# The MLP's weights kept in SBUF, the gathered rows in the freed weight buffers, weighing and gating two half steps later

## The chip, the cores and the metric

The kernel runs on one core of one Trainium2 chip. The metric is the device time of one execution in microseconds (us). Everything is float32. The engines are called by the names of the profile: PE (TensorE), DVE (VectorE), ACT (ScalarE), POOL (GpSimd) and SP (SyncE, which here only issues DMAs); the name of an engine with a q behind it is its queue.

## The reference, cut to what matters

```python
x = L0_attn_x                                     # 2 x 2048 tokens of 256 values
xn = layernorm(x)

# left branch: a Mamba mixer with an MLP behind it
h = xn + mamba_mixer(rmsnorm(xn), ...)            # 512 channels, 16 states per channel, scan over 2048 tokens
s = h + silu(rmsnorm(h) @ mlp_w1.T) @ mlp_w2.T    # mlp_w1 1024x256, mlp_w2 256x1024

# right branch: a mixture of 8 experts, two per token
p = softmax(xn @ gate_w + gate_b)
top2 = top_k(p, 2)
g = silu(sum over the two of p_e * (relu(xn @ w1[e] + b1[e]) @ w2[e] + b2[e]))

out = x + s * g
```

## The kernel before, in words

The 4096 tokens are 8 blocks of 512 (index `c`). The scan goes through 256 steps `n`: block `c`, channel group `d` (4 groups of 128 channels), pair of states `g` (8 pairs). A step has two half steps (`q` = 0 and 1). For each step DVE makes the input `b` (L1345, two states at once) and runs two scans into `h` (L1349); ACT makes the decays `da` two steps ahead (L1238) and copies the last state into `hs` (L1275); POOL multiplies `h` by `C` and, in most steps, adds the two states (L1279, L1281); PE adds up `y` three steps behind (L1251).

Around that the rest of the work is woven in by hand, half step by half step. Every engine executes its instructions in the order in which they were written out:

- `draw` gives PE about 2.0 units of other work in each half step, from generators that are asked in the order `pre`, `zs`, `projs`, `chain`, `side`. `chain` is `front`, which makes the projections, convolution and `dt` of the next block. `side` is `all_ffn`: 39 expert tiles of 256 tokens (class `Expert`), then 16 tiles of the MLP (class `Mlp`, two halves `hf` of each block), called here by the names `m0_0` to `m7_1`. A generator that yields "wait" is skipped for the half step.
- `later` holds the work of the other engines that follows on a PE result. `later.put(f, after=k)` runs `f` in `later.run()` `k` half steps later; a use that comes earlier forces it with `later.next()`.

A tile of the MLP goes like this. `run` calls `pair` four times (32 matmuls with `w1`, L854), each followed one half step later by a tanh on ACT (L1013) and again one half step later by a product on DVE (`hidm`, L1015); then `second` eight times (32 matmuls with `w2`, L866) into a PSUM bank `po`. While one tile runs, the weights of the next are loaded: four quarters of `w1` and four of `w2`, 256 KB each, from pools with five buffers (tags "w1" and "w2"). SP issues these loads, and every load waits until its buffer has been read by PE.

Each tile also needs the rows that the experts made for its 256 tokens. `gather` (called from `between`, after a `pair`) issues four indirect DMAs on POOL (L1042) into two tiles `yk`. Then `weigh` scales them with four ACT instructions (L1056) and adds the two on POOL (L1060), `tanh` runs on ACT (L1064) and `gate` on DVE (L1067). When the second matmuls are done, `total` (L1078) and, one half step later, `end` (L1085, L1086) finish the tile on DVE; `end` forces what is still open until `self.gated` holds. The next tile's `gather` comes only after that `end`.

The tiles `yk` share two buffers (tag "yk" of the pool `rows`) with the tiles `ex` that `front` uses in `exp_v` and `log_v` for the `dt` of the next block. The list `pair_of` keeps the two apart: `front` takes it from the first `exp_v` of a pair to its `log_v`, `gather` takes it until `end`, and each waits while the other has it.

Of the kernel before, what the change touches and what calls it, by code (L numbers as in the profile page):

```python
# [9 lines left out]
F32 = mybir.dt.float32  # L10
# [4 lines left out]
NB, L, DM = 2, 2048, 256  # L15
DI, DS, DR, KC = 512, 16, 16, 4
NE, FF, TOPK = 8, 1024, 2
NT = NB * L
P = 128
# [9 lines left out]
JS = TS // P  # L29
# [20 lines left out]
def kernel(  # L50
# [24 lines left out]
    wpool = ctx.enter_context(tc.tile_pool(name="w", bufs=3))  # L75
    hpool = ctx.enter_context(tc.tile_pool(name="hid", bufs=4))
    rows = ctx.enter_context(tc.tile_pool(name="rows", bufs=2))
# [99 lines left out]
    def act_table(name):  # L177

        if table[0] != name:
            nc.scalar.preload_act_table_set(name)  # L180
            table[0] = name
# [86 lines left out]
    moff, rstd, both_norms, _, _, off = (stat[:, 2 + n, :] for n in range(6))  # L268
# [84 lines left out]
    later = Later()  # L353
# [12 lines left out]
    def drop(tag, n):  # L366
        gone.setdefault(tag, set()).add(n)

    expert_rows = []
    pair_of = []  # L370
    held = []

    def ring(tag, bufs):

        n = take(tag)
        later.free(tag, n - bufs)
        return tag, n
# [432 lines left out]
    def quarter_w1(name, a1, h):  # L810
        t1 = wpool.tile([P, KM, FF // 4], F32, tag="w1", name=f"w1_{name}_{h}", bufs=5)
        nc.sync.dma_start(
            t1, a1[:, ts(h, FF // 4)].rearrange("(k p) f -> p k f", p=P)
        )
        return t1

    def quarter_w2(name, a2, h):
        t2 = wpool.tile([P, NH // 4, DM], F32, tag="w2", name=f"w2_{name}_{h}", bufs=5)
        nc.sync.dma_start(
            t2, a2[ts(h, FF // 4), :].rearrange("(c p) d -> p c d", p=P)  # L820
        )
        return t2

    class Ffn:
# [6 lines left out]
        def load_w1(self, h):  # L831
            self.w1.append(quarter_w1(self.name, self.a1, h))

        def load_w2(self, h):
            self.w2.append(quarter_w2(self.name, self.a2, h))
# [36 lines left out]
        def between(self):  # L872
            pass
# [41 lines left out]
    class Expert(Ffn):  # L915
# [6 lines left out]
        def begin(self):  # L922
            i = self.i
            e = nc.sync.value_load(expert_of[0:1, i : i + 1], min_val=0, max_val=NE - 1)
            self.a1 = w1[bass.ds(e, 1)].rearrange("o d f -> (o d) f")
            self.a2 = w2[bass.ds(e, 1)].rearrange("o f d -> (o f) d")
            self.b1 = small.tile([P, NH], F32, tag="b1", name=f"b1_{i}")
            nc.sync.dma_start(self.b1, b1[bass.ds(e, 1)].rearrange("o p c -> (o p) c"))
            self.e = e
            self.row = nc.sync.value_load(  # L930
                row_of[0:1, i : i + 1], min_val=0, max_val=NSLOT - TS
            )

        def rows(self):
            i = self.i
            self.xr = rows.tile([P, JS, DM], F32, tag="xr", name=f"xs{i}", bufs=1)
            nc.sync.dma_start(
                self.xr, xs_d[bass.ds(self.row, TS), :].rearrange("(j p) d -> p j d", p=P)
            )
            return  # L940
            yield
# [18 lines left out]
        def finish(self, po, n):  # L960
            i = self.i
            no = ring("ys", 2)
            expert_rows.append(no)
            ys = rows.tile([P, JS, DM], F32, tag="ys", name=f"ys{i}")
            later.put(
                lambda: nc.vector.tensor_tensor(
                    ys, po, self.b2.unsqueeze(1).to_broadcast([P, JS, DM]), ALU.add
                ),
                n, after=2,
            )  # L970
            later.put(
                lambda: nc.sync.dma_start(
                    ys_d[ts(i, TS), :].rearrange("(j p) d -> p j d", p=P), ys
                ),
                no, after=4,
            )

    class Mlp(Ffn):
        early = False

# [5 lines left out]

        def begin(self):
            pass

        def rows(self):  # L990

# [26 lines left out]
            later.put(tanh)  # L1018

        def between(self):  # L1020
            if not self.yk and not pair_of:
                self.gather()

        def before_second(self):
# [5 lines left out]
        def gather(self):  # L1030

            c, hf = self.c, self.hf
            i0 = c * J + hf * JS
            pair_of.append(self.name)
            yk = self.yk = [
                rows.tile([P, JS, DM], F32, tag="yk", name=f"yk{self.name}_{k}") for k in range(TOPK)
            ]
            for no in expert_rows:
                later.free(*no)
            for j in range(JS):  # L1040
                for k in range(TOPK):
                    nc.gpsimd.indirect_dma_start(  # L1042
                        out=yk[k][:, j, :], out_offset=None, in_=ys_d,
                        in_offset=bass.IndirectOffsetOnAxis(
                            ap=row_y[:, k, i0 + j : i0 + j + 1], axis=0
                        ),
                    )
            self.nxo = ring("ys", 2)
            self.xo = rows.tile([P, JS, DM], F32, tag="ys", name=f"xo{self.name}")
            self.tok = slice(c * T + hf * TS, c * T + (hf + 1) * TS)  # L1050
            nc.sync.dma_start(self.xo, x[self.tok, :].rearrange("(j p) d -> p j d", p=P))

            def weigh():
                for j in range(JS):
                    for k in range(TOPK):
                        nc.scalar.activation(  # L1056
                            yk[k][:, j, :], yk[k][:, j, :], AF.Copy,
                            scale=prob[:, k, i0 + j : i0 + j + 1],
                        )
                nc.gpsimd.tensor_tensor(yk[0], yk[0], yk[1], ALU.add)  # L1060

            def tanh():
                act_table(WITH_TANH)
                nc.scalar.activation(yk[1], yk[0], AF.Tanh)  # L1064

            def gate():
                nc.vector.scalar_tensor_tensor(yk[0], yk[1], 1.0, yk[0], ALU.add, ALU.mult)  # L1067
                self.gated = True

            later.put(weigh, after=3)  # L1070
            later.put(tanh, after=5)
            later.put(gate, after=6)

        def finish(self, po, n):
            x1, yk, xo = self.x1, self.yk, self.xo

            def total():
                nc.vector.scalar_tensor_tensor(po, po, 0.5, x1, ALU.mult, ALU.add)  # L1078
                drop("x1", self.n_x1)
                later.put(end, n)  # L1080

            def end():
                while not self.gated:
                    later.next()
                nc.vector.tensor_tensor(po, po, yk[0], ALU.mult)  # L1085
                nc.vector.tensor_tensor(xo, po, xo, ALU.add)  # L1086
                pair_of.clear()
                later.put(
                    lambda: nc.sync.dma_start(
                        out[self.tok, :].rearrange("(j p) d -> p j d", p=P), xo  # L1090
                    ),
                    self.nxo, after=3,
                )

            later.put(total)
# [338 lines left out]
```

## Time and profile before

| | us |
|---|---|
| median of 3 runs | 1565.81 |
| lowest and highest | 1560.62, 1567.42 |
| the profiled execution | 1572.91 |
| span of its trace | 1571.2 |

| engine | busy us | share of the span |
|---|---|---|
| PE | 1401.4 | 89% |
| DVE | 1247.6 | 79% |
| POOL | 1157.2 | 74% |
| ACT | 920.1 | 59% |

The profiled execution lies 7.1 us above the median, and 1.7 us of it lie outside of the span. The DMA queues moved 265.17 MB, 169 GB/s over the span. Of that the MLP's weights are 2 x 64 loads of 256 KB (33.6 MB). The first instruction of an MLP tile's matmuls starts at 1087 us; everything before is the start, the experts and the scan of blocks 0 to 5.

The shares are means over stages with different limits, and the busy time of PE is modelled, so a full PE in it is not a PE at its peak. A row of the timeline gives the start, the duration, engine, line, operation, tiles, how many instructions were merged, and in square brackets how long the engine had been idle and what ended the wait. A wait for several semaphores is put down to the last of them.

### The profile page before, as it was taken

What the parts mean: (1) busy time and instruction counts of PE and PEld (TensorE: products, weight loads), DVE (VectorE), ACT (ScalarE), POOL (GpSimd) and SP (SyncE); (2) the same over time, 40 slices, a digit from 0 to 9 for tenths busy, and PEclk for the clock granted to TensorE, in tenths of its full rate; (3) what the DMA queues carried; (4) which work ended last, traced back from release to release, by engine and by line L of the source; (5) the groups of instructions that cost most, each with busy time, mean ns of one, the idle gap of its engine ahead of it and who ended that gap; (6) DMA issues with size and microseconds to landing.
All of it is one profiled execution on the core that took longest, in us unless ns stands there. A gap on an engine that the chain in (4) does not pass through costs nothing. (4 is left out here: it accounts for less than half of the span.)

```text
span 1571.2 us, 18477 instructions
## 1 busy us (share of the span) xinstructions
PE 1401.4 (89%) x5246; PEld 985.5 (63%) x5246; DVE 1247.6 (79%) x1362; ACT 920.1 (59%) x1890; POOL 1157.2 (74%) x775
## 2 busy tenths in 40 slices
PE   5745999998999999999999999999898898799767
PEld 3532667765776667667776777667555565567536
DVE  7458898798778977799879777996898696899952
ACT  4735576567655755477657665675566564374423
POOL 2668589867886689679967887688866768677852
PEclk8557999999999999999999999999999989899988
DMA  5576335923494347724763368245832437645312
GB/s 190 187 258 252 111 120 182 327 91 102 141 321 146 96 131 250 256 88 132 234 255 110 118 213 295 87 127 180 314 105 87 143 101 249 214 131 164 96 59 84
DMA packets 203749, 265.17 MB, mean 169 GB/s; under 512 B 21744, under 2 KB 174192, under 8 KB 203648
## 3 DMA queue, kind: packets, MB, share of 16 engines
q1 hardware_dynamic: 197504, 247.21, 48.0%
q0 software_dynamic: 6144, 16.79, 3.2%
q8 instruction: 42, 0.69, 0.2%
q14 instruction: 59, 0.48, 0.1%
HBM read 227.50 MB, written 36.44 MB: 168 GB/s over the span
## 5 line engine op out<-in xcount | busy, mean ns | idle before, releaser
L1279 POOL TENSOR_TENSOR h<-h,C 128x1024 f32<-128x1024 f32 x256 | 609.9, 2384 | 246.3 <-ACT hs L1275 193.9
L1349 DVE TENSOR_TENSOR_SCAN h<-da,hs,b 128x512 f32<-128x512 f32 x384 | 479.7, 1271 | 42.6 <-PE y L1251 17.2
L1238 ACT ACTIVATE da<-dt,a_neg 128x512 f32<-128x512 f32 x512 | 358.0, 718 | 40.3 <-DVE h L1349 39.7
L1251 PE MATMUL y<-h,ident 128*128 128x512 f32 x594 | 304.6, 615 | 30.6 <-POOL h L1279 20.2
L1345 DVE TENSOR_TENSOR b<-du,B 128x1024 f32<-128x1024 f32 x256 | 314.8, 1230 | 18.0 <-DMA B<-bcd 11.1
L854 PE MATMUL phe<-xsTe,w_e 128*128 128x256 f32 x1248 | 290.4, 384 | 12.5 <-ACT hide L954 8.8
L1281 POOL TENSOR_TENSOR h<-h 128x512 f32<-128x512 f32 x215 | 277.9, 1292 | 16.9
L854 PEld LDWEIGHTS phe<-xsTe,w_e 128*128 128x128 f32 x1248 | 238.7, 192 | 80.6 <-issue 26.3
L866 PE MATMUL poe<-w_e,hide 128*128 128x256 f32 x1248 | 288.7, 380 | 0.0
L866 PEld LDWEIGHTS poe<-w_e,hide 128*128 128x128 f32 x1248 | 235.7, 190 | 64.9 <-issue 33.6
L954 ACT ACTIVATE hide<-phe,b 128x256 f32<-128x256 f32 x312 | 129.3, 469 | 128.9 <-PE phe L854 128.7
L1251 PEld LDWEIGHTS y<-h,ident 128*128 128x128 f32 x594 | 113.0, 197 | 119.6 <-issue 63.3
L1349 DVE TENSOR_TENSOR_SCAN h<-da,b 128x512 f32<-128x512 f32 x128 | 151.3, 1211 | 11.1 <-PE y L1251 3.2
L854 PE MATMUL phm<-xsTm,w_m 128*128 128x256 f32 x512 | 130.9, 410 | 22.7 <-DVE hidm L1015 19.9
L854 PEld LDWEIGHTS phm<-xsTm,w_m 128*128 128x128 f32 x512 | 104.1, 205 | 55.0 <-DVE hidm L1015 24.2
L866 PE MATMUL pom<-w_m,hidm 128*128 128x256 f32 x512 | 119.0, 384 | 2.0 <-DVE xom L1086 1.7
L866 PEld LDWEIGHTS pom<-w_m,hidm 128*128 128x128 f32 x512 | 97.7, 193 | 28.6 <-issue 11.0
L459 POOL DMA_INDIRECT xs_d<-xt,slot x64 | 63.9, 998 | 49.8 <-issue 22.2
L1275 ACT COPY hs<-h 128x2 f32<-128x2 f32 x192 | 36.1, 188 | 94.7 <-DVE h L1349 92.3
L1042 POOL DMA_INDIRECT ykm<-ys_d,row_y x64 | 61.4, 960 | 38.9 <-issue 11.7
L1015 DVE SCALAR_TENSOR_TENSOR hidm<-hidm,phm 128x512 f32<-128x512 f32 x64 | 42.7, 671 | 55.6 <-ACT hidm L1013 55.6
L582 DVE SCALAR_TENSOR_TENSOR xc<-px,par_sb,xc 128x512 f32<-128x512 f32 x96 | 71.5, 747 | 17.2 <-ACT xc L574 11.8
(175 smaller groups left out, 1431.6 us busy)
## 6 DMA issues: line engine op xcount, KB each, us to landing
w_e<-in_w SPq DMA_DIRECT2D x312, 256.0 KB
B<-bcd SPq DMA_DIRECT2D x64, 512.0 KB
C<-bcd SPq DMA_DIRECT2D x64, 512.0 KB
w_m<-in_mlp_w1T SPq DMA_DIRECT2D x64, 256.0 KB
w_m<-in_mlp_w2T SPq DMA_DIRECT2D x64, 256.0 KB
xs<-xs_d SPq DMA_DIRECT2D x39, 256.0 KB
ys_d<-ys SPq DMA_DIRECT2D x39, 256.0 KB
b<-in_b SPq DMA_DIRECT2D x39, 128.0 KB
```

The source lines that it names most:

```text
L459: r = nc.gpsimd.indirect_dma_start(out=xs_d, out_offset=bass.IndirectOffsetOnAxis(ap=slot[:, k, i : i + 1], axis=0), in_=x_of(i // J, i % ...
L582: nc.vector.scalar_tensor_tensor(v[:, s : s + T], px, conv_w[:, d, KC - 1 - s : KC - s], v[:, s : s + T], ALU.mult, ALU.add,)
L854: nc.tensor.matmul(ph[:, q, :], self.w1[c0 // 2][:, k, ts(q, P)], self.xT[:, k, :], start=(k == 0), stop=(k == KM - 1),)
L866: nc.tensor.matmul(po[:, j, :], self.hid[c // 2][:, c % 2, ts(j, P)], self.w2[c // 2][:, c % 2, :], start=(c == 0 and j == 0), stop=(c == ...
L954: nc.scalar.activation(hc[:, q, :], ph[:, q, :], AF.Relu, bias=self.b1[:, c0 + q : c0 + q + 1])
L1042: nc.gpsimd.indirect_dma_start(out=yk[k][:, j, :], out_offset=None, in_=ys_d, in_offset=bass.IndirectOffsetOnAxis(ap=row_y[:, k, i0 + j : ...
L1238: nc.scalar.activation(das[n][:, q, :], dts[c, d], AF.Exp, scale=a_neg[:, d, 2 * g + q : 2 * g + q + 1])
L1251: nc.tensor.matmul(ys[c, d], ident, hts[n][:, q, :], start=False, stop=(g == DS // 2 - 1 and q == nq - 1),)
L1279: nc.gpsimd.tensor_tensor(hts[n], hts[n], bct[c, "C", g], ALU.mult)
L1281: nc.gpsimd.tensor_tensor(hts[n][:, 0, :], hts[n][:, 0, :], hts[n][:, 1, :], ALU.add)
L1345: nc.vector.tensor_tensor(inp, dus[c, d].unsqueeze(1).to_broadcast([P, 2, T]), bct[c, "B", g], ALU.mult,)
L1349: nc.vector.tensor_tensor_scan(hts[n][:, q, :], das[n][:, q, :], inp[:, q, :], 0.0 if c % CPB == 0 else hs[c - 1][:, d, 2 * g + q : 2 * g ...
```

## The change

The MLP's eight weight quarters are loaded once, for the first MLP tile, and stay in four of the five buffers of each weight tag. All 16 tiles use them. The fifth buffer of "w1" and the fifth of "w2" become the two tiles `yk`, which are allocated once. `gather` and `end` now keep a list of their own, `yk_taken`, so that `pair_of` belongs to `front` alone. `weigh`, `tanh` and `gate` are due 5, 7 and 8 half steps after the `gather`, where they were due after 3, 5 and 6.

```diff
+    mlp_w, yk_tiles, yk_taken = ([], []), [], []
+
     class Mlp(Ffn):
...
+        def load_w1(self, h):
+            if h == len(mlp_w[0]):
+                mlp_w[0].append(quarter_w1("m", self.a1, h))
+            self.w1.append(mlp_w[0][h])
+
+        def load_w2(self, h):
+            if h == len(mlp_w[1]):
+                mlp_w[1].append(quarter_w2("m", self.a2, h))
+            self.w2.append(mlp_w[1][h])
...
         def between(self):
-            if not self.yk and not pair_of:
+            if not self.yk and not yk_taken:
                 self.gather()
...
-            pair_of.append(self.name)
-            yk = self.yk = [
-                rows.tile([P, JS, DM], F32, tag="yk", name=f"yk{self.name}_{k}") for k in range(TOPK)
-            ]
+            yk_taken.append(self.name)
+            if not yk_tiles:
+                for k in range(TOPK):
+                    yk_tiles.append(
+                        wpool.tile([P, JS, DM], F32, tag=f"w{k + 1}", name=f"yk{k}", bufs=5)
+                    )
+            yk = self.yk = yk_tiles
...
-            later.put(weigh, after=3)
-            later.put(tanh, after=5)
-            later.put(gate, after=6)
+            later.put(weigh, after=5)
+            later.put(tanh, after=7)
+            later.put(gate, after=8)
...
             def end():
                 while not self.gated:
                     later.next()
                 nc.vector.tensor_tensor(po, po, yk[0], ALU.mult)
                 nc.vector.tensor_tensor(xo, po, xo, ALU.add)
-                pair_of.clear()
+                yk_taken.clear()
```

## The prediction

> **What bounds the kernel now.** I read the page first, then a table of stages, the waits of the stage that the change touches, and the timeline where its longest wait lies. The first 1087 us hold no MLP matmul, so only the rest can change. Of the rest, the end of the scan (1510 us) parts two stages. The first two rows below are from that table (length, then busy us and instructions of PE, weight loads, DVE, ACT and POOL, then clock, DMA share and GB/s), the third is from the waits of DVE between 1087 and 1571 us.
>
> ```profile
> 1087.00:1510.00 423.00, 365.31 (x1299) 250.47 (x1298) 362.07 (x353) 220.47 (x432) 308.71 (x202) 0.93 0.49 162
> 1510.00:1571.00 61.00, 44.76 (x174) 34.70 (x174) 14.27 (x21) 17.43 (x36) 14.81 (x17) 0.86 0.19 56
> DVE hidm L1015 <- ACT hidm L1013: 55.6, 14, 13.9
> ```
>
> In the stage of 423 us DVE is busy for 362 and idle for 61. PE looks as full, but eight 128x256 matmuls take 1.73 us at full clock (the chain of waits), and 14 tiles of 64 such matmuls are then only 194 us of PE. DVE, with two scans and one product per step, paces this stage, and its idle time is what can be won. Three gaps carry it: 7.31 us at 1098 (tile m0_0), 9.66 at 1247 (m2_0), 13.87 at 1302 (m3_0). Each is put down to ACT's tanh of `hidm`. The timeline of the third, DVE first, then ACT, then POOL, shows what ACT was held by:
>
> ```profile
> 1300.74 1.27 DVE L1349 TENSOR_TENSOR_SCAN h<-da,hs,b 128x512 f32<-128x512 f32 x1
> 1315.88 0.69 DVE L1015 SCALAR_TENSOR_TENSOR hidm<-hidm,phm 128x512 f32<-128x512 f32 x1 [13.87 <-ACT hidm L1013]
> 1317.00 1.77 DVE L1067 SCALAR_TENSOR_TENSOR ykm<-ykm,ykm 128x512 f32<-128x512 f32 x1 [0.44 <-ACT ykm L1064]
> ...
> 1308.57 0.51 ACT L1056 ACTIVATE ykm<-ykm,prob 128x256 f32<-128x256 f32 x1 [10.83 <-DMA ykm<-ys_d,row_y]
> 1312.72 0.51 ACT L1056 ACTIVATE ykm<-ykm,prob 128x256 f32<-128x256 f32 x1 [2.48 <-DMA ykm<-ys_d,row_y]
> 1315.24 0.60 ACT L1013 ACTIVATE hidm<-phm 128x512 f32<-128x512 f32 x1
> ...
> 1297.52 1.27 POOL L648 TENSOR_TENSOR ls<-ex,ls 128x512 f32<-128x512 f32 x1
> 1302.85 0.99 POOL L1042 DMA_INDIRECT ykm<-ys_d,row_y  x1
> 1306.65 0.94 POOL L1042 DMA_INDIRECT ykm<-ys_d,row_y  x1 [0.30 <-issue]
> 1307.61 2.35 POOL L1279 TENSOR_TENSOR h<-h,C 128x1024 f32<-128x1024 f32 x1
> 1313.30 1.26 POOL L1060 TENSOR_TENSOR ykm<-ykm,ykm 128x512 f32<-128x512 f32 x1 [3.34 <-ACT hs L1275]
> ```
>
> The reader is to see a queue in front of a queue. POOL first does the four `dt` instructions of `log_v` (1297.5 to 1302.7), then issues four gathers (4 x 1.25 us). ACT stands before `weigh` until the rows land, the tanh of the MLP stands behind `weigh`, and DVE, in order, stands before `hidm`. m2_0 is the same picture; at m0_0 POOL was late with its products. ACT waits 38.0 us for gathered rows in this stage, 33.4 of it at these three tiles.
>
> **The change part by part.**
>
> Loads. In the written order 120 SP loads of 256 KB are gone (31.5 MB, against 162 GB/s x 423 us = 68.5 MB moved in the stage) and nothing else in number. In the waits of the stage PE never waits for a weight load; the loads come while the tile before is computed, and that covers them. DVE's only wait by that name is 1.03 us. So I count 0. They can shorten a gather: last issue to arrival took 6.04 us at 1306.65 amid loads, and 2.77 at 1560.60 with little else moving, so 0 to 3.3 us per gather. It counts only where ACT waits for rows, and after the change it mostly doesn't.
>
> Order. `pair_of` no longer parts `front` and `gather`. Half steps, as `later.now` counts them, before -> after: for m2_0 `gather` 430 -> 426, `log_v` 429 -> 427, `weigh` 433 -> 431, `end` 435 -> 433; for m3_0 `gather` 446 -> 442, `log_v` 445 -> 442, `weigh` 449 -> 447, `end` 451 -> 449. For m0_0 `gather` stays at 383, `weigh` 386 -> 388, `end` stays at 391. Now the gathers stand on POOL ahead of the four `dt` instructions, and ACT meets `weigh` five half steps (12 us or more) after them. The stalls for rows should go. What is late next is POOL: the same instructions remain to be done before the addition L1060.
>
> - m2_0. From 426 POOL has: product and addition 3.65, the second L636 1.27, four gathers 5.0, product 2.4, root 1.2, `dt` 5.1, product and addition 3.65, addition L1060 1.27. That is 23.5 us from the 1223.6 at which it starts 426 in the trace, so 1247.2, tanh 0.62, gate at about 1248. DVE would be at 433, two half steps of about 2.5 us before the 1247.1 where it stopped at 435, at about 1242.3. 5 us are left of 9.66 + 0.44.
> - m3_0. From 442 to L1060: 3.65 + 5.0 + 5.1 + 2.4 + 3.65 + 1.27 = 21, about 1 late at the start and 0.6 for the tanh: 22.6. DVE takes 7 half steps of 2.75 = 19.3. 3 us are left of 13.87 + 0.44.
> - m0_0. The rows came at 1104.75. ACT would reach `weigh` about 5 us later than the 1094.9 of before, and no `hidm` is due between 388 and 391, so the 4 to 5 us wait is covered by the two steps of `da` made ahead. But POOL was busy without a break from 1079 to 1128, and DVE cannot leave it far behind (five `h` buffers, PE's sums three steps behind). Between 0 and 7.31 left, I take 2.
>
> Won: (7.31 - 2) + (10.10 - 5) + (14.31 - 3) = 21.7 us.
>
> Later gates. `end` now finds its gate not done, besides m2_0 and m3_0 as before, at m3_1, m5_0, m5_1 and m6_1: the tanh and `gate` are forced two half steps after `weigh`, and DVE waits with the scan behind it. Nearest rows: the gate's waits on ACT were 0.43 to 0.80 us. Upper end: POOL one step behind, product and addition 3.65 + L1060 1.27 + tanh 0.62 = 5.5. I take 1 each, near the rows: -4. A new `gather` follows `end` in the same half step as before, so POOL waits no longer than before.
>
> Tail. For m7_0 `weigh` now comes at its forced `end`. ACT had the second tanh of m7_1 done at 1553.0; then four `weigh` 1.7, L1060 1.3 (with its wait 1.4), tanh 0.63, gate 0.69: 1557.5, where the gate before ended at 1556.07. The gather of m7_1 waits for it, and its rows, L1060, tanh and gate set the end (gate 0.43 behind ACT at 1565.92). -1.5.
>
> Port. `gate` reads two SBUF tiles. The timeline shows it, and `du` (L1342), at very different lengths:
>
> ```profile
> 1122.40 4.62 DVE L1342 TENSOR_TENSOR du<-dt,xc 128x512 f32<-128x512 f32 x1
> 1222.55 0.69 DVE L1342 TENSOR_TENSOR du<-dt,xc 128x512 f32<-128x512 f32 x1
> 1135.56 0.67 DVE L1067 SCALAR_TENSOR_TENSOR ykm<-ykm,ykm 128x512 f32<-128x512 f32 x1
> 1418.98 2.28 DVE L1067 SCALAR_TENSOR_TENSOR ykm<-ykm,ykm 128x512 f32<-128x512 f32 x1 [0.80 <-ACT ykm L1064]
> ```
>
> The 14 gates of the stage took 17.6 us, 1.26 each. The Trainium skill, "SBUF — State Buffer", section "Who interferes with whom", says that a DVE instruction with two SBUF inputs and a GpSimd instruction that reads SBUF cannot run together: whichever is second waits for the whole of the first. The 4.62 us lie over two products of POOL (4.67), as the rule has it. It speaks against this change, which moves the gates into a tighter schedule of POOL. By the rule at its worst, a product of 2.38 before each gate, 14 x (2.38 + 0.67 - 1.26) = -25 us, all that is won. By the trace only the chance of meeting POOL rises, from (308.7 + 12.6 of gather gaps) / 423 = 76% to 79%: -0.3 us. I take the trace, since gates met a busy POOL before as well.
>
> Sum: 21.7 - 4 - 1.5 - 0.3 = 16 us. Against the profiled execution 1572.9 - 16 = 1557; that one ran 7.1 above the median of 1565.8, which gives 1550.
>
> **The rivals.**
> - More is won: POOL's backlog doesn't hold DVE and the gates wait for nothing. 31.7 less 1.5: 1535 to 1541. For it: POOL is idle for a quarter of the stage. Against: it is full just there.
> - The gain is spent: PE's products for `y`, or `out_proj` and its x1, stop DVE instead (DVE waited 9.4 us for L762 in the stage). 0 to 7 us won: about 1562.
> - Slower: the forced gates. Six ends come two half steps behind `weigh`, each needing ACT, POOL, ACT and DVE in a row. The gross gain of 31.7 less 1.5 is gone when they cost 5.0 us each. At 7 us each (POOL a step and a half behind) 6 x 7 + 1.5 - 31.7 = +12: 1578. For it: in the stage ACT stood before the tanh four times until POOL had added. Against: those waits were 3.3 us in all, 0.9 at most.
> - That the weights are not kept is excluded by the written order, which has four loads each.
>
> **How the numbers follow.** The sum 0.62, more won 0.16, spent 0.15, slower 0.07. Half a percent, 7.8 us, is about what a measurement of this kernel can tell from no change. Faster is the first two: 0.78; same 0.15; slower 0.07. The residues (0 to 7.3 at m0_0, 1 to 5.5 for each of four gates) spread the first case over 1541 to 1558. With most of the second and third the range is 1535 to 1563.
>
> **What would show it.** ACT's wait for gathered rows in the stage falls from 38 to under 10 us; DVE's idle from 61 to about 45; its gap for `hidm` at m2_0 and m3_0 turns into waits for the tanh L1080 (L1064 before). The rate of DMA in the stage falls by almost half, with no wait of PE gone by that. The last gate comes 1.5 us later against PE's end. I'd be wrong if those gaps were still there under another name, or if forced gates waited 5 us.

## The result and the profile after

| | before | after |
|---|---|---|
| median of 14 runs each, same chip | 1561.15 us | 1551.4 us |
| lowest and highest | 1551.53, 1567.42 | 1544.34, 1554.43 |
| the profiled execution | 1572.91 us | 1551.53 us |
| its span | 1571.2 us | 1549.8 us |

The ratio of the medians is 0.9938, with a 95% interval of 0.9917 to 0.9958: the change saves 9.7 us, between 6.6 and 13.0. The two profiled executions lie 21.4 us apart, more than the change is worth: the one of before is slower than each of the 14 timed runs. The traces let the rest be set aside. I cut each into four at three instructions that both have: the first product `b`, the first MLP matmul, the end of the last scan.

| part (us) | before | after | saved |
|---|---|---|---|
| start to the first `b` | 101.4 | 86.6 | 14.9 |
| first `b` to the first MLP matmul | 985.6 | 985.5 | 0.1 |
| first MLP matmul to the end of the scan (the stage) | 424.3 | 414.2 | 10.1 |
| end of the scan to the end (the tail) | 59.9 | 63.5 | -3.6 |

The first part holds the same work in both and is no effect of the change (the eight traces of the experiments below take 86.3 to 88.0 us for it, too). What the change did is 10.1 - 3.6 = 6.5 us in this pair of executions, just under the low end of the interval.

The table of stages for both kernels, cut at the same instructions, first before and then after (columns as in the prediction: length, then busy us and instructions of PE, weight loads, DVE, ACT and POOL, then clock, DMA share, GB/s):

```profile
1087.04:1511.30 424.26, 366.56 (x1301) 251.24 (x1300) 363.37 (x354) 220.47 (x432) 308.71 (x202) 0.93 0.49 162
1072.10:1486.30 414.20, 359.53 (x1301) 246.86 (x1300) 361.35 (x354) 220.38 (x432) 307.02 (x202) 0.95 0.28 95
```

The instruction counts of the engines agree, and the rate of DMA has fallen from 162 to 95 GB/s. DVE's idle time has gone from 60.9 to 52.9 us: 8.0 of the 10.1 us are waits. The other 2.0 are DVE's own 354 instructions, which took 361.35 us where they had taken 363.37 (more on this under "Port" below). The waits of DVE in this stage, before:

```profile
DVE hidm L1015 <- ACT hidm L1013: 36.7, 7, 13.9
DVE pom L1078 <- PE pom L866: 3.3, 1, 3.3
DVE ykm L1067 <- ACT ykm L1064: 1.7, 3, 0.8
```

and after:

```profile
DVE pom L1094 <- PE pom L866: 14.3, 6, 4.5
DVE yk L1083 <- ACT yk L1080: 12.9, 5, 4.7
DVE hidm L1028 <- ACT hidm L1026: 6.9, 3, 4.7
```

The reader is to see one wait become three. 41.7 us with these names have become 34.1: the wait for `hidm` is down by 30, but 11 of it came back at `total` (L1094) and 11 at `gate` (L1083). ACT's wait for gathered rows, which was 38.0 us, is 1.9 in this stage.

Where it worked is m3_0. DVE, ACT and POOL after, in the lines that answer to those of the prediction:

```profile
1284.90 0.69 DVE L1094 SCALAR_TENSOR_TENSOR pom<-pom,x1m 128x512 f32<-128x512 f32 x1
1289.86 2.17 DVE L1083 SCALAR_TENSOR_TENSOR yk<-yk,yk 128x512 f32<-128x512 f32 x1 [3.09 <-ACT yk L1080]
...
1280.32 1.69 ACT L1072 ACTIVATE yk<-yk,prob 128x256 f32<-128x256 f32 x4
1289.20 0.63 ACT L1080 ACTIVATE yk<-yk 128x512 f32<-128x512 f32 x1 [5.87 <-POOL yk L1076]
...
1275.76 0.95 POOL L1058 DMA_INDIRECT yk<-ys_d,row_y  x1 [0.30 <-issue]
1276.73 1.29 POOL L648 TENSOR_TENSOR ls<-ex,ls 128x512 f32<-128x512 f32 x1
1287.89 1.27 POOL L1076 TENSOR_TENSOR yk<-yk,yk 128x512 f32<-128x512 f32 x1
```

The gathers now stand ahead of the `dt` instructions (L648), ACT's four `weigh` run in one piece without a wait, and what is late is POOL's addition L1076. The gap of 13.87 us is one of 3.09.

How far after is ahead of before, measured from the first MLP matmul to the `b` of each scan step, shows where the stage's 10.1 us come from:

| scan steps | what lies there | ahead at the end of it | change |
|---|---|---|---|
| 184 to 206 | m0_0, m0_1, m1_0 | 0.3 | +0.3 |
| 206 to 207 | gate of m1_1 | -4.3 | -4.6 |
| 207 to 213 | m2_0 | -0.3 | +4.0 |
| 213 to 216 | gate of m2_1 | -4.3 | -4.0 |
| 216 to 222 | m3_0 | 6.9 | +11.2 |
| 222 to the end | m3_1 to m7_0 | 10.1 | +3.2 |

(At single steps the figure also swings by several us and back, where a block of work only moved by a few steps; the rows end where such swings are small. m1_1's gate itself stands ahead of step 206 in before, where it took 0.67 us, and behind it in after. With the same work on both sides the first two rows are -0.4 and -3.9.)

One trace is one execution. The runs E4 and E7 below have the same instructions on DVE as after in this stage up to block 7, and their stages took 410.9 and 410.4 us. They agree with the table within 0.5 us but for two places of 1.7 us: the wait before `total` of m1_1 (4.49 us in after, 2.78 in both) and the gate of m2_1 (4.72 and 3.02 to 3.03). So m2_0's row reads +5.7 or +5.8 there and m2_1's -2.4, and a difference of 3 to 4 us between two single stages means nothing by itself.

### The profile page after: what moved, and what is told of

The parts are those of the page before. It is cut to its first block, busy times and chain, and to the rows that moved or that the text cites. A ratio compares the mean times of both kernels' runs of the same rounds, so it can differ in the third digit from the quotient of the medians.

```text
span 1549.8 us, 18158 instructions
## 1 busy us (share of the span) xinstructions
PE 1396.0 (90%) x5246; PEld 982.9 (63%) x5246; DVE 1244.3 (80%) x1362; ACT 919.8 (59%) x1890; POOL 1154.8 (75%) x775
## 5 line engine op out<-in xcount | busy, mean ns | idle before, releaser
L1365 DVE TENSOR_TENSOR_SCAN h<-da,hs,b 128x512 f32<-128x512 f32 x384 | 479.0, 1271 | 42.7 <-PE y L1267 17.6
L854 PE MATMUL phe<-xsTe,w_e 128*128 128x256 f32 x1248 | 290.8, 385 | 13.5 <-ACT hide L954 8.9
L1297 POOL TENSOR_TENSOR h<-h 128x512 f32<-128x512 f32 x215 | 276.4, 1286 | 16.9
L1365 DVE TENSOR_TENSOR_SCAN h<-da,b 128x512 f32<-128x512 f32 x128 | 151.2, 1210 | 11.2 <-PE y L1267 3.2
L854 PE MATMUL phm<-xsTm,w_m 128*128 128x256 f32 x512 | 125.2, 397 | 21.4 <-DVE hidm L1028 20.8
L854 PEld LDWEIGHTS phm<-xsTm,w_m 128*128 128x128 f32 x512 | 100.6, 198 | 48.9 <-DVE hidm L1028 25.9
L1058 POOL DMA_INDIRECT yk<-ys_d,row_y x64 | 61.6, 962 | 38.6 <-DVE pom L1101 21.3
L966 DVE TENSOR_TENSOR ys<-poe,b 128x512 f32<-128x512 f32 x39 | 26.6, 682 | 58.8 <-PE poe L866 51.9
```

What stands on the lines that cost most here:

```text
L854: nc.tensor.matmul(ph[:, q, :], self.w1[c0 // 2][:, k, ts(q, P)], self.xT[:, k, :], start=(k == 0), stop=(k == KM - 1),)
L1058: nc.gpsimd.indirect_dma_start(out=yk[k][:, j, :], out_offset=None, in_=ys_d, in_offset=bass.IndirectOffsetOnAxis(ap=row_y[:, k, i0 + j : ...
L1297: nc.gpsimd.tensor_tensor(hts[n][:, 0, :], hts[n][:, 0, :], hts[n][:, 1, :], ALU.add)
L1365: nc.vector.tensor_tensor_scan(hts[n][:, q, :], das[n][:, q, :], inp[:, q, :], 0.0 if c % CPB == 0 else hs[c - 1][:, d, 2 * g + q : 2 * g ...
```

## The experiments

Each is one core's whole program and is compared with the kernel before on its own chip, where that one had a median of 1561.46 us (E1 to E4) or 1561.95 us (E5 to E8). Stage and tail are cut as above.

| | median us | ratio to before, 95% | stage | tail |
|---|---|---|---|---|
| E1 weights kept, nothing else | 1560.71 | 0.9996 [0.9986, 1.0005] | 421.0 | 61.8 |
| E2 after with the delays of before | 1548.28 | 0.9911 [0.9893, 0.9929] | 412.7 | 60.7 |
| E3 after with gather and `front` coupled | 1564.78 | 1.0021 [1.0009, 1.0033] | 423.0 | 62.9 |
| E4 after with the traffic put back | 1551.87 | 0.9932 [0.9913, 0.995] | 410.9 | 63.6 |
| E5 after with less work for POOL at m0_0 | 1545.27 | 0.989 [0.9865, 0.9915] | 407.2 | 61.4 |
| E6 E2 with the mean square earlier | 1544.87 | 0.989 [0.9866, 0.9913] | 413.2 | 60.8 |
| E7 after with old delays in the last block | 1548.67 | 0.9922 [0.99, 0.9943] | 410.4 | 61.9 |
| E8 E6 with E5's edit | 1540.1 | 0.9863 [0.9837, 0.9889] | 409.6 | 60.8 |

### E1 to E4: which part of the change carries the gain

**E1**, before with the two overrides alone:

```diff
+    mlp_w = ([], [])
...
+        def load_w1(self, h):
+            if h == len(mlp_w[0]):
+                mlp_w[0].append(quarter_w1("m", self.a1, h))
+            self.w1.append(mlp_w[0][h])
...
+        def load_w2(self, h):
+            if h == len(mlp_w[1]):
+                mlp_w[1].append(quarter_w2("m", self.a2, h))
+            self.w2.append(mlp_w[1][h])
```

> Only the weights are kept: yk, pair_of and the delays 3, 5, 6 stay as before. The stage is counted from the first MLP matmul to the end of the last scan (before 424.3 us, after 414.2), the tail from there to the end (59.9 and 63.5). Theory 'order' (the gain came from moving gather and weigh): no wait of PE was for a load, so the stage stays at 421 to 425, the tail at 60, the gaps of DVE before hidm at m0_0, m2_0, m3_0 stay near 7, 10 and 14 us, time within 4 us of before. Theory 'loads' (less DMA traffic and an emptier SP queue bring the rows sooner): stage 414 to 418 and the gaps shrink to half.

Measured: no difference (0.9996). The rate of DMA in the stage is 93 GB/s, as low as in after, and the waits of before are still there. DVE at m0_0, m2_0 and m3_0 in E1:

```profile
1096.17 1.28 DVE L1027 SCALAR_TENSOR_TENSOR hidm<-hidm,phm 128x512 f32<-128x512 f32 x2 [5.44 <-ACT hidm L1025]
1248.70 0.69 DVE L1027 SCALAR_TENSOR_TENSOR hidm<-hidm,phm 128x512 f32<-128x512 f32 x1 [8.76 <-ACT hidm L1025]
```

The third was 9.96. Each is shorter than in before (7.31, 9.66, 13.87). The rows do come earlier with less traffic: from the last gather's issue to the last `weigh` of the tile it is 3.24, 2.81 and 2.77 us at these three, where it was 5.09, 3.68 and 6.07. But the order that makes ACT wait for them is unchanged, and ACT's wait for rows is still 36.5 us. E1's stage is 3.3 us shorter than before's in the two traces; by the medians, 31.5 MB of loads are worth nothing that this measurement can tell (0.75 us less, and the interval of the ratio includes 1).

**E3**, after with `gather` bound to `pair_of` again, so that kept weights and late delays remain:

```diff
-            if not self.yk and not yk_taken:
+            if not self.yk and not pair_of:
...
-            yk_taken.append(self.name)
+            pair_of.append(self.name)
...
-                yk_taken.clear()
+                pair_of.clear()
```

> After, with gather and front parted by pair_of again (yk in the fifth buffers, weights kept, delays 5, 7, 8): the delays alone. Theory 'delays carry it': the rows are there when ACT comes to weigh, stage 414 to 418. Theory 'the free gather carries it': at m2_0 and m3_0 end now forces weigh itself, so DVE waits for rows, weigh, POOL's addition and tanh in a row; stage 424 to 432, tail 63, no faster than before.

Measured: slower than before by 3.3 us (1.0021, interval above 1), and by 4.1 than E1, from which it differs in the delays and in where the rows lie. The stage, 423.0, is a little under the 424 to 432 that was expected of a free gather that carries the gain. At m2_0 and m3_0 its gates are forced behind the rows. DVE at m2_0 in E3:

```profile
1246.98 0.69 DVE L1028 SCALAR_TENSOR_TENSOR hidm<-hidm,phm 128x512 f32<-128x512 f32 x1 [5.95 <-ACT hidm L1026]
1252.12 0.69 DVE L1083 SCALAR_TENSOR_TENSOR yk<-yk,yk 128x512 f32<-128x512 f32 x1 [4.44 <-ACT yk L1080]
```

5.95 and 4.44 us are 10.4 together, where E1 loses 8.76 and 0.44: without the earlier gather the delay only divides the wait over two instructions.

**E2**, after with the three delays of before:

```diff
-            later.put(weigh, after=5)
-            later.put(tanh, after=7)
-            later.put(gate, after=8)
+            later.put(weigh, after=3)
+            later.put(tanh, after=5)
+            later.put(gate, after=6)
```

> After, with weigh, tanh and gate at 3, 5 and 6 half steps again; weights kept and gather free of front. No gate is forced but those of block 7. Theory 'delays carry it' (as the prediction had it for m0_0): ACT meets the rows too early again, 7 us at m0_0 and some 3 to 5 at m2_0 and m3_0, stage 418 to 424, tail 60, slower than after or equal. Theory 'the free gather carries it, the delays cost': the gates at m1_1, m2_1, m3_0 no longer wait behind ACT's other work, stage 404 to 412, tail 60, faster than after by 6 to 14 us.

Measured: 13.2 us under before, 3.1 under after by the medians, where the two intervals overlap. It did not become the 6 to 14 us that the second theory had forecast. So the whole gain comes from the gather that no longer waits for `front`; of the three edits, the kept weights serve to make room for it, and the two half steps bring nothing on balance. E2 does not lose what after loses at the gates of m1_1 and m2_1, but it gives the same back later: behind step 222 after gains 3.2 us on before (E4 and E7 3.2 and 3.7), and E2 loses 1.5. ACT still waits 23.7 us for rows in E2's stage, so that wait as a whole is not what costs the time.

**E4**, after with every load that it leaves out replaced by a copy of the same quarter from HBM to HBM, 120 in all, issued by SP at the same places:

```diff
+    def copy_of(w, shape, rule, **k):
+        t = dram.tile(shape, F32, tag="copy", name=f"copy{take('copy')}", bufs=16)
+        nc.sync.dma_start(t, w.rearrange(rule, **k))
...
                 mlp_w[0].append(quarter_w1("m", self.a1, h))
+            else:
+                copy_of(
+                    self.a1[:, ts(h, FF // 4)], [P, KM, FF // 4], "(k p) f -> p k f", p=P
+                )
```

(and the same for `w2`).

> After, with 120 copies of the same weight quarters from HBM to HBM in place of the 120 loads that went: SP's queue and the traffic as before (read and written), without a buffer to wait for. It computes the same. Theory 'order': rows have five half steps to arrive, so the stage stays within 3 us of after (414) and the tail within 2 of 63.5. Theory 'loads': 420 or more.

Measured: 1551.87 us, as after. The rate of DMA in the stage is back to 172 GB/s, and no time with it. With E1 this closes the question of the loads from both sides, as far as the medians can tell.

### E5 and E6: the two waits that the prediction sized or named wrongly

In after, m0_0 still loses as much as in before. DVE at m0_0, then ACT's tanh there:

```profile
1095.59 0.70 DVE L1094 SCALAR_TENSOR_TENSOR pom<-pom,x1m 128x512 f32<-128x512 f32 x1 [4.54 <-PE pom L866]
1098.59 2.16 DVE L1083 SCALAR_TENSOR_TENSOR yk<-yk,yk 128x512 f32<-128x512 f32 x1 [1.12 <-ACT yk L1080]
...
1097.93 0.63 ACT L1080 ACTIVATE yk<-yk 128x512 f32<-128x512 f32 x1 [8.10 <-POOL yk L1076]
```

PE, too, stood 3.66 us at 1089.4, before a matmul for `y` that needs POOL's L1297, with the `pom` matmuls behind it. If POOL's backlog holds all of these, taking work from POOL ahead of m0_0 must free them. **E5** leaves the addition of the two states to PE in the six steps 184 to 189, as the kernel does in other steps already:

```diff
-        return n >= 8 and not (n >= 190 and n % 2 == 0)
+        return n >= 8 and not 184 <= n < 190 and not (n >= 190 and n % 2 == 0)
```

> After, but in the six steps 184 to 189 PE adds up both states, so POOL is spared six additions L1297 (6 x 1.27 = 7.6 us) just before and in m0_0, and PE has 6 x 0.43 = 2.6 us more. Theory 'POOL's backlog held m0_0': ACT's wait of 8.10 us for L1076 falls below 3, DVE's gaps of 4.54 and 1.12 there fall by 3 to 5 us, stage 409 to 412 (after 414.2). Theory 'something else holds m0_0' (PE, or the rows): the gaps stay, stage 413 to 417.

Measured: 16.7 us under before and 6.1 under after. The stage is 7.0 us shorter than after's, more than the 2 to 5 that were expected, but only 3.7 and 3.2 shorter than E4's and E7's. ACT and DVE at m0_0 in E5:

```profile
1094.75 0.63 ACT L1080 ACTIVATE yk<-yk 128x512 f32<-128x512 f32 x1 [1.64 <-POOL yk L1076]
1096.06 0.70 DVE L1094 SCALAR_TENSOR_TENSOR pom<-pom,x1m 128x512 f32<-128x512 f32 x1 [1.46 <-DMA C<-bcd]
1097.85 0.67 DVE L1083 SCALAR_TENSOR_TENSOR yk<-yk,yk 128x512 f32<-128x512 f32 x1
```

The tanh's wait falls from 8.10 to 1.64, DVE's two gaps from 5.66 to 1.46, and at step 192 E5 is 6.0 us ahead of before, where after is level. This confirms the cause at m0_0: six additions of 1.27 us, 7.6 us of POOL's time. Not all of it stays won. At steps 195 and 196 DVE waits 2.37 and 2.85 us for PE's L762 (`out_proj`), where all others wait 2.57 us once, and by step 206 E5 is 3.9 us ahead.

At m2_0 the gap in after stands before `hidm`, where the prediction put it at the gate. DVE, ACT and POOL in after:

```profile
1227.00 0.69 DVE L1028 SCALAR_TENSOR_TENSOR hidm<-hidm,phm 128x512 f32<-128x512 f32 x1 [4.68 <-ACT hidm L1026]
...
1223.39 0.20 ACT L802 ACTIVATE rms<-rms 128x4 f32<-128x4 f32 x1 [5.42 <-POOL rms L800]
1226.37 0.60 ACT L1026 ACTIVATE hidm<-phm 128x512 f32<-128x512 f32 x1
...
1222.17 0.94 POOL L1058 DMA_INDIRECT yk<-ys_d,row_y  x1 [0.30 <-issue]
1223.13 0.22 POOL L800 TENSOR_SCALAR rms<-rms 128x4 f32<-128x4 f32 x1
```

`log_v` of a block also calls `root`, whose first instruction (L800, four numbers per partition) runs on POOL and whose second (L802) runs on ACT. The gathers that were moved ahead of `log_v` stand on POOL in front of those 0.22 us, ACT waits 5.42 us for them, and the tanh of `hidm` stands behind ACT. **E6** is E2 with L800 issued when the squares of the block are complete, at `store` (the line numbers of the code behind it are 10 higher):

```diff
                     nc.sync.dma_start(x1d[c][:, ts(hf, JS), :], xn)
...
+                elif hf:
+                    mean_square(c)
...
+    def mean_square(c):
+        ss, ms = (rms[:, n, c * J : (c + 1) * J] for n in range(2))
+        nc.gpsimd.tensor_scalar(ms, ss, 1.0 / DM, RMS_EPS, ALU.mult, ALU.add)
+        mean_made.add(c)
...
     def root(c):
+        if c not in mean_made:
+            mean_square(c)
         ss, ms, r, tmp = (rms[:, n, c * J : (c + 1) * J] for n in range(4))
-        nc.gpsimd.tensor_scalar(ms, ss, 1.0 / DM, RMS_EPS, ALU.mult, ALU.add)
```

> The kernel with the old delays (weights kept, free gather), and the mean square of the MLP's norm (L800 on POOL) issued when the block's x1 is stored instead of in log_v. Theory 'at m2_0 ACT stands in log_v for L800, which stands on POOL behind the gathers': ACT's wait of 5.41 us and DVE's gap of 4.54 before hidm go, stage from 412.7 to 407 to 410. Theory 'POOL has too much to do there anyway': the same time is lost at the gate of m2_0 instead, stage 412 to 414.

Measured: 17.1 us under before. It is 3.4 under E2, where the two intervals overlap, and the stage is 413.2, no shorter than E2's 412.7, as the second theory had it. ACT and DVE at m2_0 in E6:

```profile
1227.20 0.63 ACT L1090 ACTIVATE yk<-yk 128x512 f32<-128x512 f32 x1 [5.13 <-POOL yk L1086]
...
1220.31 0.69 DVE L1038 SCALAR_TENSOR_TENSOR hidm<-hidm,phm 128x512 f32<-128x512 f32 x1 [0.48 <-ACT hidm L1036]
1227.86 2.16 DVE L1093 SCALAR_TENSOR_TENSOR yk<-yk,yk 128x512 f32<-128x512 f32 x1 [3.02 <-ACT yk L1090]
```

The wait for L800 is gone and the gap before `hidm` is 0.48 instead of E2's 4.54. But ACT now reaches the tanh of the gate early and stands 5.13 us before POOL's addition, and DVE waits 3.02 at the gate: the wait that the prediction had expected here was hidden under the other. At step 213 E6 is 2.2 us ahead of E2, and by the end of the stage nothing of it is left. What time E6's trace does win lies before the stage: from the first `b` to the first MLP matmul it takes 981.7 us, E8 the same, and the eight other traces 985.5 to 992.4. Those eight lose 2.5 to 3.3 us to E6 between scan steps 40 and 56 (E8 1.3), where each of them holds the same wait for L800, of 4.42 us (and a second of 4.41 to 4.43 some 170 us later). ACT, and then DVE behind it, in E2:

```profile
372.30 0.20 ACT L802 ACTIVATE rms<-rms 128x4 f32<-128x4 f32 x1 [4.42 <-POOL rms L800]
...
373.91 1.28 DVE L1365 TENSOR_TENSOR_SCAN h<-da,hs,b 128x512 f32<-128x512 f32 x1 [2.25 <-ACT da L1254]
```

In E6 neither wait is there. But E8, which has the same edit, still loses 1.3 us between these steps, so at most 1.2 to 2.0 us there are the edit's. At m2_0, for which it was made, it won nothing that was left at the end of the stage; that it won something in the earlier blocks is likely but not shown.

### E7 and E8: the tail, and a better version

**E7** gives the tiles of block 7 alone the old delays:

```diff
+            late = 0 if c == NBLK - 1 else 2
-            later.put(weigh, after=5)
-            later.put(tanh, after=7)
-            later.put(gate, after=8)
+            later.put(weigh, after=3 + late)
+            later.put(tanh, after=5 + late)
+            later.put(gate, after=6 + late)
```

> After, with the old delays for the last block's two tiles alone. Theory: the tail of after is longer since weigh comes late for m7_0, and then PE stands 3.02 instead of 1.74 us and does its last 32 matmuls at a lower clock in 10.06 instead of 7.17 us: tail 60 to 61 (after 63.5, before 59.9), those 32 matmuls in about 7.2, stage as after, time 2 to 4 us less. Rival (the longer tail is chance): tail 63.

PE's last matmuls before, after and in E7:

```profile
1557.59 7.17 PE L866 MATMUL pom<-w_m,hidm 128*128 128x256 f32 x32 [1.74 <-DVE xom L1086]
```

```profile
1533.85 10.06 PE L866 MATMUL pom<-w_m,hidm 128*128 128x256 f32 x32 [3.02 <-DVE xom L1102]
```

```profile
1531.27 7.17 PE L866 MATMUL pom<-w_m,hidm 128*128 128x256 f32 x32 [1.74 <-DVE xom L1103]
```

The later gate of m7_0 holds its `end`, and with it the PSUM bank that these 32 matmuls need, for 1.28 us more; and in after they then take 2.89 us longer. With the old delays both are as before. The tail is 61.9 us against 63.5, not the 60 to 61 that was expected, and the median is 2.7 us under after's (the intervals overlap). The six kernels with the pause of 1.74 us have tails of 59.9 to 61.9, so of the tail only these 32 matmuls, 1.28 and 2.89 us, are shown to be the delays' work. The stage was to be as after's and is 3.8 shorter, with the same instructions up to block 7: that is the spread of single traces.

**E8** puts E6 and the edit of E5 together (E2's delays, `mean_square` at `store`, and `not 184 <= n < 190` in `paired`).

> Old delays, free gather, weights kept, early mean square, and PE adding both states in steps 184 to 189. If both backlogs are real: stage 403 to 408, tail 60, 1541 to 1546 us, ratio 0.984 to 0.989. If the waits only move: stage 410 to 413 and a time like that with the old delays alone.

Measured: 1540.1 us, the lowest median here: 21.9 us under before and 11.3 under after, both clear of the intervals. E5's and E6's intervals overlap with its own, so that the two edits add up is not shown. Its stage, 409.6, fits neither of the two forecasts (403 to 408, 410 to 413): of the 6.0 us that E5 wins by step 192 only 1.6 are found here. ACT and DVE at m0_0 in E8:

```profile
1080.93 0.51 ACT L1082 ACTIVATE yk<-yk,prob 128x256 f32<-128x256 f32 x1 [5.08 <-DMA yk<-ys_d,row_y]
...
1084.86 1.28 DVE L1038 SCALAR_TENSOR_TENSOR hidm<-hidm,phm 128x512 f32<-128x512 f32 x2 [5.43 <-ACT hidm L1036]
```

With the old delays ACT meets `weigh` before the rows have landed, and DVE's gap before `hidm` is that of E1 (5.44). At this one tile, then, the two half steps are needed once POOL is free. At m2_0 and m3_0 they are not: from step 207 to 213 E8 gains 4.4 us on before and from 216 to 222 11.5.

## Why the prediction was right, and where its steps failed

The direction held, and so did the mechanism at m2_0 and m3_0: with the gather free of `front`, DVE no longer stands there for the rows, and POOL is what is late next. E1 to E4 show that this, and not the loads, carries the gain. The time, 1551.4 us against 1550, came out close by luck: the gain was 9.7 us and not 16, and the starting median had been 4.7 too high (1565.8 from 3 runs, 1561.15 from 14). In the trace the sum 5.3 + 5.1 + 11.3 - 4 - 1.5 - 0.3 became 0.3 + 4.0 + 11.2 - 8.6 - 3.6, and 3.2 that was not in it: 6.5. Term by term:

- **Loads, 0.** Right within what the medians can tell; E1 and E4 show it.
- **m3_0, 14.31 to 3 left.** Right: 3.09, and 11.2 us gained over its steps.
- **m2_0, 10.10 to 5 left at the gate.** The size was right by luck (4.68 + 1.02), the place and the cause wrong. The step "root 1.2" counted `root` as work of POOL only. Its first instruction has ACT waiting behind the gathers that were moved past it, and E6 shows that this wait covered the one that was counted, of which 3.02 us come out when the first is gone.
- **m0_0, 7.31 to 2 left.** Failed. 4.54 + 1.12 were left, and at step 192 nothing had been won. The text had POOL busy without a break from 1079 to 1128 and took 2 in spite of it, on the ground that buffers keep DVE near. They do not keep the addition L1076 near: it stands behind POOL's products and additions in order, and E5 shows that these were the cause. It is the largest single miss: 5.3 us counted, 0.3 at most won up to step 206 (the gate itself also took 2.16 us, where it had taken 1.39).
- **Forced gates, 4 us in all at m3_1, m5_0, m5_1, m6_1.** Failed in place and in size. None of the four waited. Two that were not on the list did: m1_1, where the later tanh falls behind two table loads and four silu instructions of `front` (2.98 us at the gate), and m2_1, where it falls behind the ten instructions of `exp_v`, 1255.99 to 1262.28 (4.72 us at the gate, 3.02 and 3.03 in E7 and E4). The list was made from the order of `end` against `gate` alone; what else ACT has in the two half steps was not looked up. They cost 4.6 and 4.0 us by the steps, 8.6 where 4 had been counted (7.9 without the gate's own 0.67 us; 7.0 and 7.1 in E4 and E7). E2 has no wait at either gate.
- **Behind step 222, not in the sum: +3.2.** These are not waits. DVE's idle time there is 15.9 us in after and 13.5 in before, although m4_0's wait for `hidm` of 2.41 us became 0.47. What is shorter are the instructions that read two SBUF tiles: four `du` took 4.2 us where they had taken 7.2, and seven gates 7.4 where they had taken 9.7. E4, E5 and E7 have the same sums within 0.1, and E2, E6 and E8, with the old delays, have gates of 11.0 to 11.5. So the two half steps also win some 3.6 us here, which is part of why they cost nothing on balance.
- **Tail, -1.5.** The direction was right, the size too small by 2.1 in this trace: PE's start is 1.28 late, as counted, and the matmuls themselves slowed by 2.89 (see below).
- **Port, -0.3.** For the gates the direction was right and the size too small: 18.8 us after and 17.6 before, a loss of 1.2. But `du` had been left out of the sum, and it went the other way by more. The rows of the stage, gates and `du`, before and then after:

```profile
L1067 DVE SCALAR_TENSOR_TENSOR ykm<-ykm,ykm 128x512 f32<-128x512 f32 x14 | 17.6, 1255 | 1.7 <-ACT ykm L1064 1.7
L1342 DVE TENSOR_TENSOR du<-dt,xc 128x512 f32<-128x512 f32 x8 | 17.5, 2190 | 0.0
L1083 DVE SCALAR_TENSOR_TENSOR yk<-yk,yk 128x512 f32<-128x512 f32 x14 | 18.8, 1343 | 12.9 <-ACT yk L1080 12.9
L1358 DVE TENSOR_TENSOR du<-dt,xc 128x512 f32<-128x512 f32 x8 | 13.8, 1730 | 0.0
```

In after, every row of these two that is longer than 0.70 us starts while POOL has a TENSOR_TENSOR running, and ends 0.54 to 0.56 us behind the end of it (in one case, the `du` of 5.09 us at 1106.93, behind the second of two products). The gate of m3_0, 2.17 us from 1289.86, starts under this product:

```profile
1289.12 2.36 POOL L1295 TENSOR_TENSOR h<-h,C 128x1024 f32<-128x1024 f32 x1
```

That agrees with the rule of the Trainium skill's "SBUF — State Buffer", section "Who interferes with whom". Its worst case (-25 us) did not come; in this pair of traces the gates and `du` together took 2.5 us less.

- **DVE's idle 61 to about 45** was 52.9: m0_0, the two unlisted gates and longer waits before `total`.

Of the rivals, "more is won" asks for what E5 and E8 do by taking work from POOL; "the gain is spent" did not come in after (DVE's wait for L762 is 9.1 us, where it was 9.4), but it is what takes part of E5's gain back at step 196; "slower" comes nearest in E3, where the delays come without the earlier gather, with 4.44 and 4.37 us at two gates.

What stays open: the same instructions between the first `b` and the first MLP matmul took 985.5 to 992.4 us in the eight traces without the early mean. Some of the differences between single spans are of this kind, and stages with the same instructions differ by 3 to 4 us. So the verdicts above are taken from the medians, and causes from single waits that more than one trace shows.

## What to carry to other kernels

When a step is moved on an in-order queue, list for every instruction that it passes which other engine waits for it, however small it is: 0.22 us of POOL behind four gathers made ACT wait 5.4. When a step is made later, look up what its engine does in the half steps it moves into. And a wait that is taken away may have covered another of nearly the same length; a run with only that wait removed tells.

## What the runs showed of the hardware

The granted PE clock fell near the end of after. The table of windows, while the last 32 matmuls run: 1560 to 1565 before, 1535 to 1540 after; then two windows of the pause ahead of them in after:

```profile
1560.00:1565.00 5.00, 4.76 (x23) 3.84 (x21) 0.20 (x1) 2.03 (x4) 2.28 (x3) 1.00 0.30 82
1535.00:1540.00 5.00, 5.00 (x14) 3.99 (x13) 0.00 (x0) 1.67 (x4) 2.46 (x3) 0.53 0.46 140
1530.80:1532.80 2.00, 0.04 (x1) 0.00 (x0) 1.12 (x3) 1.11 (x2) 0.15 (x1) 1.00 0.00 0
1532.90:1533.80 0.90, 0.00 (x0) 0.00 (x0) 0.87 (x3) 0.00 (x0) 0.45 (x1) 0.50 0.00 0
```

The granted clock was 0.53, and PE did 14 matmuls in the 5 us against 23. PE had paused for 3.02 us, from 1530.83 to 1533.85, and the clock fell to 0.50 some 2 us into the pause. Of the four kernels with that pause, after and E4 took 10.06 and 10.08 us for the 32 matmuls, E3 8.86 and E5 7.17; all six with 1.74 us took 7.17. The Trainium skill, "TensorE: Matmul & The Clock Gate", section "Part 1: The HAM clock gate", tells of a free-running window of about 3.4 us, and half the clock after an idle one. That the same pause costs 2.9, 1.7 or 0 us fits a window that runs free of the kernel. But here the clock fell after 2 us without a matmul, less than a whole idle window; how much idle time is enough, no run here settles.

In the opening of before's profiled execution POOL's gathers, which elsewhere there wait 0.30 us for their issue, stand twice for 5.4 us, at 64.04 and here:

```profile
89.58 1.46 POOL L459 DMA_INDIRECT xs_d<-xt,slot  x1 [5.37 <-issue]
```

DVE is 6.8 us behind after's by 61 us, 10.7 by 75 and 15.1 by 87. The nine other traces reach the first `b` at 86.3 to 88.0 us, this one at 101.4. The cause stays open; it is a reason to cut a span into parts before its difference is explained.
